# Pacing the preparation of a batch by the steps of the batch before it

## The chip, the core and the metric

The kernel runs on one core of a Trainium2 chip. The metric is device time in microseconds (us); lower is better. A time is the median of several runs; the profile is of one more execution of the same program.

## The reference: what is computed

The input is x of shape 4 x 128 x 64 x 64: four batches, 128 channels, 4096 positions, in float32. Two layers follow each other.

Layer 0 normalizes x in groups, derives offsets and a mask for 9 taps per position from a 3 x 3 convolution, samples the image bilinearly at the offset places (a deformable convolution), multiplies with a weight, and adds the result to x.

Layer 1 treats the 4096 positions as tokens of 128 features. After a layer norm, each of 16 heads of width 8 forms cosines and their running products; these features are query, key and value at once:

```python
scores = jnp.einsum('bhsd,bhtd->bhst', q, q) / np.sqrt(D)
attn = jax.nn.softmax(scores, axis=-1)
ctx = jnp.einsum('bhst,bhtd->bhsd', attn, q)
```

A projection, a small feed-forward network and a mixture of 8 experts (2 taken per token) follow, each with a residual. Batches don't depend on each other. Within a batch, attention needs the features of all its positions.

## The kernel before

**The main work is a list of steps.** The 16 heads are 4 groups of 4, the 4096 queries 8 chunks of 512, the 4096 keys 32 tiles of 128. A run is one batch, group and query chunk; a step is one key tile of a run. `scores` (line 1170) issues four matmuls (L1178, PE) into two PSUM tiles `sc` and two exponentials (L1187, ACT) from there into two tiles `e`. `context` (line 1191) multiplies `e` with the values into the accumulator `acc` (L1195, PE). Scores are issued two steps ahead of the context (`LAG`). Tag `sc` has 3 buffers of two PSUM banks, tag `e` has 6 in SBUF, which is three steps. Scores of two chunks against each other are symmetric, so some `e` tiles are transposed on DVE (`turn`, L1069), stored, loaded as `et` and used in a later run (L1131) in place of new scores. There are 964 steps for batch 0, and 4 x (8 x 32 - 7 x 4) = 912 for each of batches 1 to 3, so 3700 in all, with 7400 exponentials; the batches end at steps 964, 1876, 2788 and 3700 (`of_batch`, line 1260).

**Beside the steps run three kinds of jobs**, written as Python generators. "prepare" (line 785) makes a batch ready: group norm, a table of image corners in DRAM, offsets, then `deform` (line 563), and with it `convolved` and `features`, which are also named "prepare". "finish" (line 1012) does all that follows attention for one chunk. "turned" adds the `et` products. The generators run at build time: each `yield need(pe, dve, lat, ...)` (line 197) says what the next piece will cost on PE and DVE and how long to wait after it. `Beside` (line 62) is a planner with its own clock, which advances 1.82 us per step (`STEP`); at each step it takes pieces from its queue, sorted by rank (lowest first), until the planned PE credit (0.44 us per step, at most one PE piece per step) or the DVE backlog (3.2 us, or 0.4 near the end of a run) is used up. The order it finds is the order of the instructions on PE, DVE, SP and POOL, which each run theirs in that order. ACT holds the exponentials and few others. A `yield` itself emits no instruction.

**`deform` works through 96 units**: 8 chunks of positions x 3 groups of taps x 4 blocks of 128 positions. A unit takes a tile `v` that three indirect DMAs on POOL (L575) have gathered (three `v` buffers; two units are gathered ahead), multiplies and adds it on DVE (L589, L591, L592), transposes three blocks on DVE into `tr` (L617), and issues the gathers of the unit after next. The four units of a tap group share a `tr` tile, which lies in one of the three buffers `st` that `turn` uses too; after the fourth, four DMAs on SP store it (`smd<-tr`). After 12 units, `convolved` loads the chunk again (12 DMAs `sT<-smd` on SP) and multiplies it with the weight in 18 PE pieces (`conv_ps`, L273), and `features` writes keys, queries and values to DRAM. `progress[b]` (line 584) is 0.1 + 0.9 x the share of units begun.

**What orders "prepare" against the rest.** When a batch begins, "prepare" of the next is added, with `begun` the step at which that happens (lines 1371 to 1374); for batch 1 it is a step of batch 0 after the preparation of batch 0 itself, near step 288. At each step the main loop (line 1330) compares `progress` of the coming batch with `share`, the part of the steps that have passed out of those up to 80 before the batch's end, and sets the rank of all "prepare" jobs:

```python
share = (n - begun) / (of_batch[b] - 80 - begun)
beside.rank("prepare", 2 if progress.get(b + 1, 0.0) > share else 0.5)
```

"finish" has rank 1 (a second one beside it 2) and "turned" -1. So a preparation that is ahead of its share comes behind "finish", and one that is late comes before it; one that is ahead still runs whenever there is room. On the first step of a batch's last run, all that is left of "prepare" is emitted at once (`drain`, line 1379). `force` (line 156) takes "prepare" pieces when no score can be issued because keys are missing.

**When "finish" has work.** Batches 0 and 1 run group by group over all 8 chunks, so a chunk is complete only in the last quarter of the batch; much of "finish" falls into the next batch. Batch 2 is in two halves of 4 chunks and batch 3 goes chunk by chunk (`LOTS`, line 44).

Of the kernel before, what the change touches and what calls it, by code (L numbers as in the profile page):

```python
# [196 lines left out]
def need(pe=0.0, dve=0.0, lat=0.0, hold=False, after=0.0):  # L197

    return pe, dve, lat, hold, after


def ve(n, ops=1):

    return ops * (0.17 + n / 960.0)
# [6 lines left out]
def tr(n):  # L213

    return 0.13 + 0.115 * n
# [3 lines left out]
def kernel(  # L219
# [37 lines left out]
    prepared = {}  # L257

    progress = {}
    featuring = []  # L260


# [2 lines left out]
    def misc(name):  # L265
        if alone:
            return ps_s.tile([P, 2, 512], F32, tag="sc", name=name)[:, 0, :]
        return ps_m.tile([P, 512], F32, tag="misc", name=name)
# [294 lines left out]
    def deform(b, tab, idx, wt):  # L563


        AHEAD = NV - 1
        units = [
            (ch, kg, j) for ch in range(NCH) for kg in range(3) for j in range(4 * ch, 4 * ch + 4)
        ]

        def gather(_, kg, j):
            v = work.tile([P, 3, 4 * C], F32, tag="v", name=f"v{b}_{j}_{kg}", bufs=NV)
            for k in range(3):
                kk = 3 * kg + k
                nc.gpsimd.indirect_dma_start(  # L575
                    out=v[:, k, :], out_offset=None, in_=tab,
                    in_offset=bass.IndirectOffsetOnAxis(ap=idx[:, j, kk : kk + 1], axis=0),
                )
            return v, beside.gathered()

        sent = 0.0
        ahead = [gather(*units[n]) for n in range(AHEAD)]
        for n, (ch, kg, j) in enumerate(units):
            progress[b] = 0.1 + 0.9 * n / len(units)
            v, landed = ahead.pop(0)
            v4 = v.rearrange("p k (q c) -> p (k q) c", c=C)
            w12 = wt[:, j, 3 * kg : 3 * kg + 3, :].rearrange("p k q -> p (k q)")
            yield need(dve=ve(1536), after=landed)
            nc.vector.tensor_tensor(v4, v4, w12[:, :, None].to_broadcast([P, 12, C]), ALU.mult)  # L589
            yield need(dve=ve(768) + ve(384))  # L590
            nc.vector.tensor_tensor(v[:, :, : 2 * C], v[:, :, : 2 * C], v[:, :, 2 * C :], ALU.add)  # L591
            nc.vector.tensor_tensor(v[:, :, :C], v[:, :, :C], v[:, :, C : 2 * C], ALU.add)  # L592
            if (b, ch) == (0, 0):

                if (kg, j) == (0, 0):
                    sT = big.tile([P, KK, CH], F32, tag="xs", name="sT_first")
                yield need(pe=tr(3), dve=ve(384))
                pt = misc(f"sT_ps{j}_{kg}")
                for k in range(3):
                    nc.tensor.transpose(pt[:, P * k : P * (k + 1)], v[:, k, :C], ident)  # L600
                nc.vector.tensor_copy(
                    sT[:, 3 * kg : 3 * kg + 3, P * j : P * (j + 1)],
                    pt[:, : 3 * P].rearrange("p (k c) -> p k c", c=P),
                )
                if n + AHEAD < len(units):
                    beside.later(beside.dve, lambda u=units[n + AHEAD]: ahead.append(gather(*u)))
                if (kg, j) == (2, 3):
                    featuring.append(True)
                    beside.add("prepare", convolved(b, ch, sT), 0.5, True)
                continue  # L610

            yield need(dve=ve(384))
            if j % 4 == 0:
                beside.flush(sent)
                tr9 = work.tile([P, 4, 4, 4, 32], F32, tag="st", name=f"tr{b}_{ch}_{kg}", bufs=NST)
            for k in range(3):
                nc.vector.transpose(  # L617
                    out=tr9[:, k, :, j % 4, :],
                    in_=v[:, k, :C].rearrange("p (c i) -> p c i", i=32),
                )  # L620
            if n + AHEAD < len(units):
                beside.later(beside.dve, lambda u=units[n + AHEAD]: ahead.append(gather(*u)))
            if j % 4 < 3:
                continue
            while kg == 0 and len(featuring) > 1:
                yield need(lat=1.0)

            def put(ch=ch, kg=kg, tr9=tr9):
                for o in range(4):
                    nc.sync.dma_start(  # L630
                        out=smd[ch % 2][:, 3 * kg : 3 * kg + 3, :, o].rearrange(
                            "i k c n -> i (k c) n"
                        ),
                        in_=tr9[32 * o : 32 * (o + 1), :3].rearrange("p k c j t -> p (k c) (j t)"),
                    )

            sent = beside.dve
            beside.later(sent, put)
            if kg == 2:

                while featuring:
                    yield need(lat=1.0)
                featuring.append(True)
                beside.later(
                    beside.dve + 0.1,
                    lambda ch=ch: beside.add("prepare", convolved(b, ch), 0.5, True),
                )
        while featuring:
            yield need(lat=1.0)
# [135 lines left out]
    def prepare(b):  # L785
        xs = big.tile([P, KK, CH], F32, tag="xs", name=f"xc{b}")
        xc = xs.rearrange("p k n -> p (k n)")[:, :NPOS]
        for i in range(4):
            nc.sync.dma_start(
                out=xc[:, 1024 * i : 1024 * (i + 1)], in_=xf[b, :, 1024 * i : 1024 * (i + 1)]  # L790
            )
        tab = tabs[b % NTAB]
        if b == 1:
            borders(tab, nc.sync)
        yield need(lat=8.0)
        got = []
        yield from group_norm(b, xc, got)
        yield from corner_table(b, xc, *got, tab)
        idx = work.tile([P, NBLK, KK], I32, tag="idx", name=f"idx{b}", bufs=1)
        wt = work.tile([P, NBLK, KK, 4], F32, tag="wt", name=f"wt{b}", bufs=1)  # L800
        yield from offsets(b, xc, idx, wt)
        if b == 0:
            settle()
        yield from deform(b, tab, idx, wt)
# [289 lines left out]
    def granted(emit):  # L1094
        if room[0]:
            room[0] -= 1
            emit()
        else:
            asking.append(emit)
# [7 lines left out]
    def fetch(run, kt):  # L1107
        giver = takes[run]
        g, par = runs[giver][1], runs[giver][2] % 2
        if (g, par, kt) in turning:  # L1110
            beside.flush()
        e = turned_tile(run, kt)
        nc.sync.dma_start(
            out=e.rearrange("p r h x -> p (r h x)"),
            in_=etd[g][par][kt].rearrange("p r x -> p (r x)"),
        )
        fetched[run, kt] = e, beside.now + 16.0
# [44 lines left out]
    def load_queries(run):  # L1162
        b, g, sc = runs[run][:3]
        if run not in queries and (b, sc) in prepared:
            q = work.tile([P, CH], F32R, tag="qT", name=f"qT{run}", bufs=3)
            nc.sync.dma_start(out=q.bitcast(F32), in_=qTd[b % 2][sc][P * g : P * (g + 1)])
            queries[run] = q
            landing[run] = beside.now + 4.0
# [91 lines left out]
    of_batch = {runs[i][0]: ends[i + 1] for i in range(len(runs))}  # L1260
# [4 lines left out]
    for n, (run, t) in enumerate(steps):  # L1265
        b, g, sc = runs[run][:3]
# [54 lines left out]
    n = issued = begun = 0  # L1321
    beside.rate = 1.0
    with tc.manual_schedule(engines={PE, DVE, SP, POOL}):
# [6 lines left out]
        while n < len(steps):  # L1330
# [11 lines left out]
            b, g, sc, ts, kind = runs[run]  # L1342
# [10 lines left out]
                backlog = 0.4 if at >= len(ts) - 3 else 3.2  # L1353
            if b + 1 < NB:

                share = (n - begun) / (of_batch[b] - 80 - begun)
                beside.rank("prepare", 2 if progress.get(b + 1, 0.0) > share else 0.5)
            beside.step(backlog)
            if issued <= n + LAG and issued < len(steps) and at_hand(issued, n):
# [2 lines left out]
            if t == ts[0]:  # L1362
# [8 lines left out]
                if not beside.has("prepare") and b + 1 < NB and (b + 1, 0) not in prepared:  # L1371
                    beside.rate = beside.RATE
                    begun = n
# [2 lines left out]
                beside.drain("turned")  # L1376
            if following:
                if following[0] != b and at == 0:
                    beside.drain("prepare")

                if at == 1:
                    load_queries(run + 1)
                    if len(ts) <= 8 and run + 2 < len(runs):
                        load_queries(run + 2)
                if run + 1 in takes and at == len(ts) - 5:
                    for kt in range(4):
                        granted(lambda r=run + 1, kt=kt: fetch(r, kt))
# [91 lines left out]
```

## Time and profile before

| | |
|---|---|
| time before, median of 3 runs | 7759.71 us (7757.02 to 7764.04) |
| profiled execution | 7737.5 us |
| its span, first to last instruction | 7735.7 us |
| mean granted TensorE clock | 0.964 |
| PE busy | 7156.1 us, 93% |
| ACT busy | 6871.2 us, 89% (of it the exponentials 6868.1) |
| DVE busy | 4484.8 us, 58% |
| POOL busy | 1648.3 us, 21% (of it the gathers 1444.7) |

Busy time is the union of an engine's instructions; the busy time of PE is modelled from pipelined matmuls, so it is no measure of how much room PE has. A group line of the profile names line, engine, operation, what is written and read, the count, the busy time and the mean duration, and behind the bar the idle time of the engine just before those instructions and what ended most of it. A window line gives start and end in us from the span's start, its length, then for each engine asked for the busy time and the count, the granted TensorE clock (1.00 is full speed), the busy share of the 16 DMA engines and GB/s.

### The profile page before, as it was taken

What the parts mean: (1) busy time and instruction counts of PE and PEld (TensorE: products, weight loads), DVE (VectorE), ACT (ScalarE), POOL (GpSimd) and SP (SyncE); (2) the same over time, 40 slices, a digit from 0 to 9 for tenths busy, and PEclk for the clock granted to TensorE, in tenths of its full rate; (3) what the DMA queues carried; (4) which work ended last, traced back from release to release, by engine and by line L of the source; (5) the groups of instructions that cost most, each with busy time, mean ns of one, the idle gap of its engine ahead of it and who ended that gap; (6) DMA issues with size and microseconds to landing.
All of it is one profiled execution on the core that took longest, in us unless ns stands there. A gap on an engine that the chain in (4) does not pass through costs nothing.

```text
span 7735.7 us, 181988 instructions
## 1 busy us (share of the span) xinstructions
PE 7156.1 (93%) x73700; PEld 2517.5 (33%) x73700; DVE 4484.8 (58%) x9000; ACT 6871.2 (89%) x7441; POOL 1648.3 (21%) x1326
## 2 busy tenths in 40 slices
PE   2579999899999999999999989989999999999997
PEld 1122232323333333333333323333333333333333
DVE  7666456666444767776554667765444545545444
ACT  0478999888999899989999988988999999999995
POOL 5454134343000432422000333431000000000000
PEclk6789999999999999999999999999999999999998
DMA  5777567978556878887766788997665587777762
GB/s 175 207 229 229 145 202 236 306 240 282 162 169 198 277 226 269 280 268 247 206 177 184 236 259 281 295 296 248 183 188 161 150 253 242 245 236 253 240 216 76
DMA packets 928758, 1735.41 MB, mean 224 GB/s; under 512 B 169458, under 2 KB 398348, under 8 KB 877228
## 3 DMA queue, kind: packets, MB, share of 16 engines
q1 hardware_dynamic: 828062, 1417.20, 60.4%
q0 software_dynamic: 92160, 302.06, 12.1%
q8 instruction: 578, 9.47, 0.5%
q10 hardware_dynamic: 7694, 4.52, 0.2%
q14 instruction: 264, 2.16, 0.1%
HBM read 1061.47 MB, written 661.93 MB: 223 GB/s over the span
## 4 chain that ended last, share of the span: by engine, by line
PE 81%; DMA 7%; DVE 4%; issue 2%; ACT 2%; SPq 2%; another core or an unknown queue 0%; POOL 0%; ACTq 0%; POOLq 0%; DVEq 0%
PE acc L1195 39%; PE sc L1178 24%; PE acc L1131 5%; PE e_ps L273 4%; PE conv_ps L273 3%; ACT e L1187 2%; PE f_ps L273 2%; DMA sT<-smd 1%; DMA et<-etd 1%; PE om_ps L507 1%; DMA etd<-st 1%; DVE v L589 1%; DMA kT<-kTd 1%; DMA qT<-qTd 1%; PE ao_ps L273 1%
## 5 line engine op out<-in xcount | busy, mean ns | idle before, releaser
L1187 ACT ACTIVATE e<-sc 128x1024 f32<-128x1024 f32 x7400 | 6868.1, 1068 | 724.7 <-PE sc L1178 470.2
L1195 PE MATMUL acc<-e,qf 128*32 128x512 f32 x29600 | 3961.1, 605 | 27.0 <-DVE cu L1399 16.2
L1178 PE MATMUL sc<-qT,kT 32*128 32x512 f32 x14800 | 2390.7, 500 | 292.4 <-ACT e L1187 153.6
L1178 PEld LDWEIGHTS sc<-qT,kT 32*128 32x128 f32 x14800 | 956.3, 183 | 3697.6 <-ACT e L1187 3078.1
L575 POOL DMA_INDIRECT v<-tab,idx x1152 | 1444.7, 1254 | 1754.5 <-DVE tr L617 1108.1
L1069 DVE STREAM_TRANSPOSE st<-e 128x1024 f32<-128x1024 f32 x792 | 937.4, 1222 | 775.5 <-ACT e L1187 606.5
L1195 PEld LDWEIGHTS acc<-e,qf 128*32 128x32 f32 x29600 | 800.4, 110 | 587.7 <-issue 329.1
L376 POOL TENSOR_TENSOR r<-ln_t,expo 128x4 f32<-128x4 f32 x96 | 112.2, 1169 | 3135.1 <-DVE ln_t L374 3096.3
L589 DVE TENSOR_TENSOR v<-v,wt 128x1536 f32<-128x1536 f32 x384 | 666.0, 1734 | 91.3 <-DMA v<-tab,idx 63.2
L1131 PE MATMUL acc<-et,qf 128*32 128x128 f32 x12672 | 521.3, 281 | 36.4 <-DMA et<-etd 30.5
L993 DVE TENSOR_TENSOR eo<-e_ps,gt 128x512 f32<-128x512 f32 x256 | 175.1, 685 | 549.6 <-PE e_ps L273 544.2
L273 PE MATMUL conv_ps<-sT,wconv_sb 128*32 128x256 f32 x4464 | 365.9, 402 | 26.4 <-DMA sT<-smd 17.9
L1131 PEld LDWEIGHTS acc<-et,qf 128*32 128x32 f32 x12672 | 302.4, 110 | 236.8 <-issue 187.1
L591 DVE TENSOR_TENSOR v<-v 128x768 f32<-128x768 f32 x384 | 367.9, 958 | 10.5
L1397 DVE COPY cu<-acc 128x512 f32<-128x512 f32 x128 | 88.5, 691 | 413.7 <-PE acc L1195 372.0
L617 DVE STREAM_TRANSPOSE tr<-v 128x128 f32<-128x128 f32 x1116 | 257.7, 282 | 40.4 <-DMA etd<-st 25.1
L592 DVE TENSOR_TENSOR v<-v 128x384 f32<-128x384 f32 x384 | 215.5, 561 | 13.3
L376 POOL TENSOR_TENSOR rstd<-lt_t,expo 128x4 f32<-128x4 f32 x32 | 57.7, 1804 | 533.2 <-DVE lt_t L374 526.2
L273 PE MATMUL f_ps<-w_sb,h 128*32 128x128 f32 x4096 | 164.8, 280 | 0.0
L878 DVE TENSOR_SCALAR h<-h_ps,b_sb 128x512 f32<-128x512 f32 x128 | 95.0, 744 | 102.5 <-PE h_ps L876 99.1
L273 PEld LDWEIGHTS conv_ps<-sT,wconv_sb 128*32 128x32 f32 x4464 | 91.4, 109 | 170.1 <-issue 151.3
L754 POOL COPY fx<-rn 128x512 f32<-128x512 f32 x32 | 28.9, 904 | 528.9 <-DVE rn L753 328.1
(224 smaller groups left out, 3041.1 us busy)
## 6 DMA issues: line engine op xcount, KB each, us to landing
etd<-st SPq DMA_DIRECT2D x1584, 256.0 KB
et<-etd SPq DMA_DIRECT2D x396, 1024.0 KB
kT<-kTd SPq DMA_DIRECT2D x400, 256.0 KB
smd<-tr SPq DMA_DIRECT2D x372, 192.0 KB
sT<-smd SPq DMA_DIRECT2D x372, 192.0 KB
qf<-fqd SPq DMA_DIRECT2D x400, 144.0 KB
qT<-qTd SPq DMA_DIRECT2D x166, 256.0 KB
atd<-cu SPq DMA_DIRECT2D x128, 256.0 KB
```

The lines of the kernel that those rows point to most:

```text
L273: nc.tensor.matmul(dst[c : c + 32], lhsT=lhsT[:, c : c + 32], rhs=rhs, start=start, stop=stop)
L575: nc.gpsimd.indirect_dma_start(out=v[:, k, :], out_offset=None, in_=tab, in_offset=bass.IndirectOffsetOnAxis(ap=idx[:, j, kk : kk + 1], ax ...
L589: nc.vector.tensor_tensor(v4, v4, w12[:, :, None].to_broadcast([P, 12, C]), ALU.mult)
L591: nc.vector.tensor_tensor(v[:, :, : 2 * C], v[:, :, : 2 * C], v[:, :, 2 * C :], ALU.add)
L592: nc.vector.tensor_tensor(v[:, :, :C], v[:, :, :C], v[:, :, C : 2 * C], ALU.add)
L617: nc.vector.transpose(out=tr9[:, k, :, j % 4, :], in_=v[:, k, :C].rearrange("p (c i) -> p c i", i=32),)
L993: nc.vector.tensor_tensor(ws[hf], pe.rearrange("p (e c) -> p e c", c=C), gt[:, i, 4 * hf : 4 * (hf + 1), None].to_broadcast([P, 4, C]), AL ...
L1069: nc.vector.transpose(out=st[:, :, 2 * pr : 2 * pr + 2, :].rearrange("p o h (q j) -> p o (h q) j", j=32), in_=es[pr].rearrange("p h (q o i ...
L1131: nc.tensor.matmul(acc[32 * h : 32 * (h + 1), P * kt : P * (kt + 1)], lhsT=qf[:, t, QW * h : QW * h + 32], rhs=e[:, :, h, 32 * t : 32 * (t ...
L1178: nc.tensor.matmul(ps[i // 2][:, i % 2, :], lhsT=kT[h : h + 32, P * (t % 4) : P * (t % 4 + 1)], rhs=qT[h : h + 32, :], start=True, stop=True,)
L1187: nc.scalar.activation(e, ps[pr], AF.Exp, scale=1.0 / math.sqrt(HD))
L1195: nc.tensor.matmul(acc[32 * h : 32 * (h + 1), :], lhsT=qf[:, t % 4, QW * h : QW * h + 32], rhs=es[h // 2][:, h % 2, :], start=(t == ts[0]) ...
```

## The change

A list `due` of one number is added. At each step the main loop writes the current `share` into it, and `share` now counts up to 200 steps before the end of the batch in place of 80. At the head of each unit, `deform` of batches 1 to 3 asks whether its progress is more than 0.06 above `due[0]`; while it is, it yields a piece without work that is ready again 1.5 us later on the planner's clock. Before the draining at the last run of a batch, `due[0]` is set to 1.

```diff
     progress = {}
+
+    due = [1.0]
     featuring = []
...
         for n, (ch, kg, j) in enumerate(units):
             progress[b] = 0.1 + 0.9 * n / len(units)
+            while b and progress[b] > due[0] + 0.06:
+                yield need(lat=1.5)
             v, landed = ahead.pop(0)
...
             if b + 1 < NB:

-                share = (n - begun) / (of_batch[b] - 80 - begun)
+                share = (n - begun) / (of_batch[b] - 200 - begun)
+                due[0] = share
                 beside.rank("prepare", 2 if progress.get(b + 1, 0.0) > share else 0.5)
...
                 if following[0] != b and at == 0:
+                    due[0] = 1.0
                     beside.drain("prepare")
```

## Prediction

> **What bounds the kernel now.** I read the page first: which engine is filled, and when.
>
> ```profile
> span 7735.7 us, 181988 instructions
> ...
> ACT  0478999888999899989999988988999999999995
> ...
> L1187 ACT ACTIVATE e<-sc 128x1024 f32<-128x1024 f32 x7400 | 6868.1, 1068 | 724.7 <-PE sc L1178 470.2
> ```
>
> ACT has 7400 exponentials at 6868.1 / 7400 = 0.928 us, 1.856 us per step, and little else. After the start the time is therefore 1.85 us per step plus whatever ACT idles. ACT's row in the slices drops from 9 to 8 in three places; the windows of the exponentials (start:end, length, ACT busy, count, clock, DMA share, GB/s) say how much:
>
> ```profile
> 987.00:2007.00 1020.00, 910.85 (x980) 0.97 0.81 251
> 2007.00:2292.00 285.00, 284.43 (x309) 1.00 0.56 165
> 2292.00:3668.00 1376.00, 1257.60 (x1353) 0.98 0.81 251
> 3668.00:4105.00 437.00, 436.32 (x473) 1.00 0.65 187
> 4105.00:5384.00 1279.00, 1126.65 (x1209) 0.98 0.84 261
> 5384.00:7600.00 2216.00, 2204.05 (x2385) 1.00 0.70 214
> ```
>
> Length minus busy is ACT's idle time: 109.2, 0.6, 118.4, 0.7, 152.4 and 12.0 us. The same windows for the units' first multiplication (L589) have 96, 0, 96, 0, 96 and 0 of them: ACT idles only while a preparation is under way, 380 us in three stages, which I call stages 1, 2 and 3 (for batches 1, 2 and 3). "finish" and the turned products do it no harm alone.
>
> Next, who holds ACT up in stage 3 (the waits of ACT in that window: total, times, longest):
>
> ```profile
> ACT e L1187 <- PE acc L1195: 65.1, 57, 2.7
> ACT e L1187 <- PE sc L1178: 55.8, 46, 5.2
> ```
>
> PE, in two ways. The timeline shows the first:
>
> ```profile
> 4474.73 1.94 ACT L1187 ACTIVATE e<-sc 128x1024 f32<-128x1024 f32 x2 [1.16 <-PE acc L1195]
> ...
> 4476.24 0.64 PE L273 MATMUL conv_ps<-sT,wconv_sb 128*32 128x256 f32 x8
> ...
> 4476.70 1.04 PE L1195 MATMUL acc<-e,qf 128*32 128x512 f32 x8
> ...
> 4477.84 1.94 ACT L1187 ACTIVATE e<-sc 128x1024 f32<-128x1024 f32 x2 [1.16 <-PE acc L1195]
> ```
>
> A step takes 4477.84 - 4474.73 = 3.11 us, because the exponential starts when `acc` of two steps earlier ends (4476.70 + 1.04 = 4477.74). It lasts some steps, costs about 1.2 us each, and is gone. Counted over the trace, starts within 0.2 us after that end hold 45, 46 and 66 us of the three stages' idle time. My reading, an inference: with three steps' worth of `e` this happens when a turned `e` is freed late because DVE's queue is deep. The rest are late scores behind PE's waits for DMAs and DVE.
>
> **How near the limit lies.** The new head of a unit emits no instruction: the program keeps its 181988 instructions in another order. Unit k (0 to 95) may begin when 0.1 + 0.9 k/96 <= (n - begun)/(end - 200 - begun) + 0.06. For stages 2 and 3, begun and end are 912 steps apart, so n >= begun + 712 x (0.04 + 0.009375 k) = begun + 28 + 6.675 k. Where the units stand now follows from the first and last start of L589 (1062.9 and 1926.0; 2491.6 and 3602.5; 4324.5 and 5290.9) and half the exponentials counted up to there:
>
> - Stage 1: begun about 288, 476 steps in place of 712, so unit 0 from step 307 and unit 95 from 731. Now they run at 718/2 = 359 and 359 + 815/2 = 766: some 35 steps or more behind the limit. It never binds. No "finish" work exists before the last quarter of batch 0, so the rank decides nothing: **0 us**.
> - Stage 2: begun 964. Unit 0 runs at 964 + 204/2 = 1066 (limit 992), unit 95 at 1066 + 1080/2 = 1606 (limit 1626). Only the last chunks bind, by up to 20 steps.
> - Stage 3: begun 1876. Unit 0 at 1876 + 226/2 = 1989 (limit 1904), unit 36 at 1989 + 328/2 = 2153 (limit 2144), unit 95 at 2153 + 558/2 = 2432 (limit 2538). From about unit 36 the limit binds, and at the end the preparation is 106 steps later, still 250 steps ahead of the batch; no draining, no forced pieces.
>
> **What the moved work meets.** Held are, for some 60 units of stage 3: three POOL gathers each (1.25 us), 1.74 + 0.95 + 0.56 + 3 x 0.28 = 4.1 us of DVE, every fourth unit 4 SP stores, and per chunk 12 SP loads, 144 `conv_ps` matmuls and the DVE work of the features. Nothing on an engine's queue waits for a held unit, as the hold is in the order and not on the chip; SP and POOL get these DMAs later among the others, each behind the DVE work that it stores or frees, as now; the held buffers are two `v` (nobody else's by then) and one of three `st`, now for 3 x 6.7 = 20 steps in place of 14, and stage 2 already holds it 17. DVE's idle time before turning in stage 3 for a store of `tr` was 33.3 us over 160 transposes and is not ACT's: I take 0, and 33 us as the bad end.
>
> The price of the pace comes from comparing stages. These are the windows of ACT for units 0 to 35 and 36 to 95, stage 3 and then stage 2:
>
> ```profile
> 4324.00:4680.00 356.00, 305.88 (x328) 0.97 0.84 263
> 4680.00:5291.00 611.00, 520.73 (x558) 0.97 0.90 290
> 2491.00:2916.00 425.00, 380.59 (x410) 0.98 0.80 251
> 2916.00:3602.00 686.00, 623.37 (x671) 0.98 0.88 277
> ```
>
> | | steps per unit | ACT idle | per unit | per step |
> |---|---|---|---|---|
> | stage 3, first 36 | 4.6 | 50.1 us | 1.39 | 0.31 |
> | stage 3, last 60 | 4.65 | 90.3 us | 1.50 | 0.32 |
> | stage 2, first 36 | 5.7 | 44.4 us | 1.23 | 0.22 |
> | stage 2, last 60 | 5.6 | 62.6 us | 1.04 | 0.19 |
>
> Stage 1, with 96 units in 407 steps (4.2 each), idled 105.0 us there, 1.09 per unit, but had no "finish" beside it. So idle time is neither fixed per step nor quite per unit. At the slower pace it is lower per unit. For the 60 held units, then 6.4 steps apart, I take stage 2's 1.04 in place of 1.50: 62.6 - 90.3 = **-28 us**. Bounds: no gain per unit, 0; no idle time left at all, -90. The 106 steps into which the work moves have ACT full now (91.27 of the 93 us after 5291) and must take part of this idle time; the per-unit figure contains that.
>
> Rank: with 200, a preparation counts as late for longer, so in stage 2 it goes before "finish" more often (unit 12 is at its share at step 1115, under the old rule at 1141). "finish" then ends later, and the stretch after it, 3668 to 4105 with 0.7 us idle, hides that. I take 0; if the cover were gone, the price is the difference between the parts of stage 2, (1.23 - 1.04) x 36 = 7 us either way.
>
> Sum: 0 + 0 - 28 + 0 = -28 us: 7737.5 - 28 = 7709.5 for the profiled execution, which is 22 us under the median shown; on the median 7759.7 - 28 = **7732 us**, -0.36%.
>
> Two rules of the Trainium skill speak against more than that. The gap of 1.16 us repeats exactly; "Perfetto Trace Analysis", section "Optimization Strategy", says consistent bubbles can mean too few buffers for the next tile. By that rule the gaps would follow the turned tiles, whose number stays, and the gain would be 0. The clock rows are 0.97 in 4680 to 5291 and 1.00 after; "TensorE: Matmul & The Clock Gate", section "HAM oscillation — how this bites in real kernels", says that idle gaps of PE above about 3.4 us throttle it again. If a longer stage kept 0.97, 106 steps at 1.86 us would lose 3%, 6 us, and the sum would be -22.
>
> **The rivals.**
>
> 1. *The idle time is per unit, and the order is only dealt anew.* For it: stage 1, the fastest, has no more per unit than stage 2. Against: stage 3 has 40% more. Gives 0, with some 10 us either way from the new order.
> 2. *Slower: the idle time is per step that a preparation is alive.* Each step then has turning, stores and a deep DVE queue beside it; "finish" takes the DVE room that held units leave, since the planner fills its backlog with any ready job. Price: 106 steps x 0.32 + 20 x 0.19 = +38 us, in stage 3 between steps 2153 and 2538, so 7798. It decides if held units idle more than 90.3 / 385 = 0.23 us per step; stage 2 measured 0.19, stage 3 0.32. For it: most idle time is with `conv_ps` or `et` on PE, which remain. Against: stage 2.
> 3. *A larger gain.* The planner's backlog stays low whenever a unit is held, turned tiles are freed in time, and the 3.11 us steps go: up to -90, so 7670.
> 4. *The change doesn't do what it says*: the limit doesn't bind. True of stage 1 and most of stage 2; for stage 3 the step numbers exclude it. It belongs with rival 1.
>
> **How the numbers follow.** This kernel's measurement can tell about 0.2%, 15.5 us, from no change. Forecast (-16 to -60): 0.38. Larger gain (rival 3): 0.12. Rivals 1 and 4: 0.27. Rival 2: 0.23. So faster 0.50, same 0.27, slower 0.23. Likeliest own range 7700 to 7744. The range takes in most of rivals 2 and 3: 7670 to 7803; the 33 us for `st` lies within it.
>
> **What would show it.** The first 2000 us as before. In stage 3, L589 from about 4325 to 5470, unit starts 6.7 steps apart, POOL's gathers thinned out likewise; ACT idle in the last 60 units near 60 us; steps of 3.11 us fewer in stage 3 and as many in stage 2. Wrong: idle time per unit of 1.5 or more at the slower pace, idle time of ACT after 5500 us or between 3668 and 4105, or stage 1 changed.

## The result, and the profile after

| | before | after |
|---|---|---|
| median of 20 runs each | 7751.22 us (7734.60 to 7772.24) | 7775.64 us (7760.84 to 7802.88) |
| ratio after / before, 95% interval | | 1.0033 (1.0025 to 1.0041) |
| profiled execution | 7737.5 us | 7776.7 us |

The changed kernel is 24 us slower; 7732 was forecast. The profiled execution of before lies 14 us under its median and that of after on its own, so the two traces are 39 us apart, 15 more than the medians; a second pair, below, is 48 us apart. First the page of after:

```profile
span 7774.9 us, 181967 instructions
...
ACT  0478999888999898889999988889999999999995
...
L1191 ACT ACTIVATE e<-sc 128x1024 f32<-128x1024 f32 x7400 | 6867.8, 1067 | 769.0 <-PE sc L1182 504.9
```

The exponentials take what they took (6868 us); ACT's idle time before them has grown from 724.7 to 769.0 us, so all of it is waiting. Which stage? The windows of ACT after, cut at the same steps as those shown of before (320, 810, 964, 1640, 1876, 2480), the last one cut again at step 2800:

```profile
992.00:2016.00 1024.00, 911.14 (x983) 0.98 0.80 250
2016.00:2306.00 290.00, 284.81 (x312) 0.99 0.55 163
2306.00:3704.00 1398.00, 1257.99 (x1360) 0.98 0.80 249
3704.00:4148.00 444.00, 436.15 (x476) 0.99 0.63 179
4148.00:5410.00 1262.00, 1126.49 (x1216) 0.97 0.82 254
5410.00:6016.00 606.00, 592.04 (x644) 1.00 0.65 198
6016.00:7643.00 1627.00, 1612.59 (x1759) 1.00 0.73 225
```

Length minus busy: 112.9, 5.2, 140.0, 7.9, 135.5, 14.0, 14.4 us, against 109.2, 0.6, 118.4, 0.7, 152.4 and, for what is now two windows, 12.0. The pace came as computed: in stage 3 the units stand 6.57 steps apart from unit 36 on (4.73 before), and the last L593 (the units' first multiplication, L589 before) starts at step 2538, 5531 us. Stage 3 moved 17 us of idle time out of its first part (8 in a second pair of traces) and has 14 back in the next window, which had none. **The loss is in stage 2**, where I had put 0: 22 us in its main window and 7 in the one behind it.

The waits of ACT in stage 3 (4148 to 5540), against 65.1 and 55.8 us before, say that the kinds of waiting are the same:

```profile
ACT e L1191 <- PE acc L1199: 63.2, 53, 2.6
ACT e L1191 <- PE sc L1182: 51.4, 52, 6.0
```

**How far one trace goes.** Between steps 320 and 810 the order is the same in both kernels and in most of those below; ACT's idle time there was 109 and 121 us in two traces of before, 113 and 131 in two of after, and up to 132 in others. Traces of one and the same order thus lie up to 23 us apart there, and a difference below some 20 us in one stage of one trace is no finding by itself. The experiments ran on several chips, which fall into two kinds: on some the kernel before takes 7749 to 7777 us (that of the result too, and those of the first eight runs below), on others 7610 to 7613. Between the kinds only ratios to the kernel before on the same chip are compared.

### The profile page after: what moved, and what is told of

Same layout as the page of the kernel before. It is cut to its first block, busy times and chain, and to the rows that moved or that the text cites. A ratio compares the mean times of both kernels' runs of the same rounds, so it can differ in the third digit from the quotient of the medians.

```text
span 7774.9 us, 181967 instructions
## 1 busy us (share of the span) xinstructions
PE 7182.2 (92%) x73700; PEld 2520.8 (32%) x73700; DVE 4481.9 (58%) x9000; ACT 6871.1 (88%) x7441; POOL 1602.5 (21%) x1326
## 4 chain that ended last, share of the span: by engine, by line
PE 82%; DMA 6%; DVE 4%; ACT 3%; issue 2%; SPq 2%; another core or an unknown queue 0%; ACTq 0%; POOL 0%; POOLq 0%; DVEq 0%
PE acc L1199 40%; PE sc L1182 24%; PE acc L1135 5%; PE conv_ps L275 4%; PE e_ps L275 3%; ACT e L1191 3%; PE f_ps L275 2%; DMA et<-etd 1%; PE om_ps L509 1%; DMA sT<-smd 1%; DMA qT<-qTd 1%; DMA etd<-st 1%; DVE v L593 1%; DVE st L1073 0%
## 5 line engine op out<-in xcount | busy, mean ns | idle before, releaser
L1191 ACT ACTIVATE e<-sc 128x1024 f32<-128x1024 f32 x7400 | 6867.8, 1067 | 769.0 <-PE sc L1182 504.9
L577 POOL DMA_INDIRECT v<-tab,idx x1152 | 1393.3, 1209 | 1872.3 <-DVE tr L621 1191.6
L593 DVE TENSOR_TENSOR v<-v,wt 128x1536 f32<-128x1536 f32 x384 | 666.7, 1736 | 91.6 <-DMA v<-tab,idx 68.3
```

The lines of the kernel that those rows point to most:

```text
L577: nc.gpsimd.indirect_dma_start(out=v[:, k, :], out_offset=None, in_=tab, in_offset=bass.IndirectOffsetOnAxis(ap=idx[:, j, kk : kk + 1], ax ...
L1191: nc.scalar.activation(e, ps[pr], AF.Exp, scale=1.0 / math.sqrt(HD))
```

## The experiments

In the tables, "stage 2" and "stage 3" are ACT's idle time (us) in steps 964 to 1876 and 1876 to 2800, the quieter steps behind a preparation included; "end" is 2800 to 3700, "tail" the time from the last exponential to the last instruction. All these are counted over the traces.

**Which part of the change?** Four kernels on one chip (before: 7748.8 us); end220 and a second trace of before and of after on another (before: 7777.3).

hold_alone: the hold as in the change, the rank by 80 as before.

```diff
-share = (n - begun) / (of_batch[b] - 200 - begun)
-due[0] = share
+share = (n - begun) / (of_batch[b] - 80 - begun)
+due[0] = (n - begun) / (of_batch[b] - 200 - begun)
```

> The hold as in the change, but the rank of the preparation still by the share up to 80 steps before the end. Three theories of the 25 us that the change costs. Rank: in stage 2 the preparation now goes before the finishing work, and this is what costs; then stage 2 idles 114 to 120 us on ACT as before and the kernel is within 10 us of before. Alive: idle time is paid per step that a preparation lives; then the same life gives +20 to +30 us. Order: the time hangs on which pieces happen to meet in the new order; then stage 2 and stage 3 may each differ from before and from the change by 10 to 25 us, without a rule.

stage3_alone: hold and rank only for the preparation in stage 3.

```diff
-share = (n - begun) / (of_batch[b] - 200 - begun)
-due[0] = share
+share = (n - begun) / (of_batch[b] - (200 if b == 2 else 80) - begun)
+due[0] = share if b == 2 else 9.0
```

> Rank and hold changed for the preparation of batch 3 alone; batches 1 and 2 as before. Rank: within 10 us of before, since stage 3 was never ranked differently for long. Alive: +20 to +35 us, as the 106 added steps are all in stage 3. Order: stage 2 equal to that of before (118 us idle on ACT, within 8), stage 3 within 20 us of that of before, so -15 to +20 in all.

end80: both, with 80 for 200, so the hold binds harder (units of stage 3 are 7.8 steps apart) and binds in stage 1 too (5.6 in place of 4.4). end220: with 220.

```diff
-share = (n - begun) / (of_batch[b] - 200 - begun)
+share = (n - begun) / (of_batch[b] - 80 - begun)     # end220: 220
```

> The hold with the old 80 in place of 200 in the share, so that the units of stages 2 and 3 are 7.8 steps apart and the preparations end 130 and 220 steps later than before. Alive: 130 x 0.19 + 220 x 0.27 = +80 us or more over before. Per unit (the forecast's rival 1): 0 to +25 us. The forecast's own mechanism (less idle time per unit at a slower pace): below 0. Rank: the rank rule is that of before, so near 0.

> The change with 220 in place of 200: the units of stages 2 and 3 are 6.5 steps apart in place of 6.7, and all pieces meet anew. If the time follows the pace (200: +25 us, 80: -7 to -15), it is at +25 to +30. If it follows the chance of the order, it lies anywhere from -20 to +35, and probably not within 5 us of the change.

slack07: the margin 0.07 in place of 0.06.

```diff
-            while b and progress[b] > due[0] + 0.06:
+            while b and progress[b] > due[0] + 0.07:
```

> The change with 0.07 in place of 0.06, which moves the limit of each unit some 7 steps earlier. Alive and rank: within 6 us of the change, so +18 to +32 us over before. Order: another order, so it may lie 10 to 25 us from the change on either side, with other steps slow.

before_again and after_again: the two kernels unchanged.

> The kernel before once more, for a second profile. It says how far two executions of one program differ in each stage. If the stages' idle times on ACT (109, 118 and 152 us) come back within 5 us, a difference of 20 us between two programs in one stage means something; if they scatter by 20 us, it does not.

> The changed kernel once more, for a second profile. In the first one, from the start of batch 1 to step 1876 ACT idled 30 us more than in the kernel before, and in stage 3 about as much. If the order of stage 2 is the cause, its surplus of 20 us or more comes back; if it was chance of one execution, it shrinks under 10 us.

| | ratio to before | stage 2 | stage 3 | end | tail |
|---|---|---|---|---|---|
| before, two traces | 1 | 119, 129 | 153, 150 | 11, 14 | 80, 81 |
| after, two traces | 1.0033 (1.0025 to 1.0041) | 148, 160 | 150, 156 | 15, 17 | 76, 75 |
| hold_alone | 1.0041 (1.0026 to 1.0056) | 124 | 167 | 9 | 103 |
| stage3_alone | 1.0000 (0.9990 to 1.0009) | 124 | 147 | 14 | 81 |
| end80 | 0.9980 (0.9968 to 0.9993) | 115 | 109 | 15 | 137 |
| slack07 | 1.0013 (1.0003 to 1.0024) | 127 | 159 | 3 | 89 |
| end220 | 0.9988 (0.9977 to 0.9998) | 146 | 141 | 4 | 80 |

What follows: paced in stage 3 alone, the change neither costs nor gains. The slowest pace, end80, is the fastest kernel, so a slower pace as such does not cost: my rival 2, idle time per step that a preparation is alive, is out. A gain below the kernel before is what the forecast's own mechanism said of end80; that one order was run at this pace, so the pace and the luck of its order are not told apart. Neither does the rank decide by itself: with the rank of before (hold_alone) stage 2 is as before and the kernel loses 32 us elsewhere; slack07 has the rank of 200 and, in its one trace, a good stage 2 too; and end220, 20 steps from the change, turns +24 us into -9. That the rank plays a part in stage 2 is not excluded: in the table, the kernels ranked by 200 or 220, all but slack07, have more idle time there than those ranked by 80. The small steps from 0.06 to 0.07 and from 200 to 220 move the time as much as the change did, without direction. The planner finds another order each time.

**Is it the deep DVE queue?** shallow_dve is the kernel before with DVE's backlog at 1.6 in place of 3.2, after my inference that turned `e` are freed late.

```diff
-backlog = 0.4 if at >= len(ts) - 3 else 3.2
+backlog = 0.4 if at >= len(ts) - 3 else 1.6
```

> The kernel before with the planner's limit on the DVE backlog at 1.6 us in place of 3.2; nothing else. My theory of the 3.11 us steps is that a turned tile is freed late behind a deep DVE queue, so that an exponential gets the buffer of two steps earlier and waits for acc. With a shallower queue such waits must become fewer: from 160 us of idle time in the three stages to 110 us or less, and the time falls by 30 to 60 us if nothing else gets late. If the repeated gap only comes from having six e buffers, it stays near 160 us.

7920.73 us, ratio 1.0181 (1.0167 to 1.0195), where 30 to 60 us less was expected. ACT's waits for `acc` did fall, from 157.5 to 91.5 us, which supports the inference; but those for `sc` rose from 470.2 to 571.9, and the tail from 80 to 215 us, most of the loss; I put that down to "finish", which finds less room beside the steps. The deep queue costs waits and buys more than they cost.

**What is lost in stage 2.** Most gaps of ACT of 2.5 us or more sit at the same steps in each trace of the changed kernel: 9 of the 11 in stage 2 come back in its second trace (3 of 5 in those of before). In stage 2 they sum to 26.0 and 35.4 us before, and to 56.1 and 64.7 after, 30 us more: the loss. At step 1127 the timeline of after reads (lines not needed are left out):

```profile
2619.71 0.34 SPq L1117 DMA_DIRECT2D et<-etd  x1
...
2622.20 0.52 SPq L1034 DMA_DIRECT2D a<-rdd  x1
...
2629.26 1.08 PE L1135 MATMUL acc<-et,qf 128*32 128x128 f32 x16 [4.56 <-DMA et<-etd]
2629.62 0.69 DVE L833 TENSOR_TENSOR aT<-aT,a 128x512 f32<-128x512 f32 x1 [14.20 <-DMA a<-rdd]
...
2630.11 1.94 PE L1199 MATMUL acc<-e,qf 128*32 128x512 f32 x8
...
2634.22 2.33 DVE L1073 STREAM_TRANSPOSE st<-e 128x1024 f32<-128x1024 f32 x2
...
2635.52 4.90 ACT L1191 ACTIVATE e<-sc 128x1024 f32<-128x1024 f32 x5 [8.72 <-DVE st L1073]
```

Two loads issued 2.5 us apart are used 9.5 and 7.4 us after their issue, as soon as they have landed. PE's next piece waits for `et` (4.56 us), with `acc` and the next scores behind it. DVE's next piece, a "finish" multiplication that the planner allows 6 us after the issue of `a`, has waited 14.20 us, with turning and the multiplications of a unit behind it; the turned `e` comes free at 2635.5, and ACT has stood 8.72 us.

The windows of PE there show two things that the timeline does not (after the busy time and the count: the granted clock, the share of the DMA engines, GB/s):

```profile
2619.70:2629.20 9.50, 5.01 (x68) 0.95 1.05 317
2628.30:2635.00 6.70, 5.74 (x52) 0.50 0.29 109
```

From the issue of `et` to its use the 16 DMA engines were busy throughout (share 1.05, which can pass 1 as a packet counts where it begins; 0.80 over the stage's main window), and the granted clock of PE fell to half, from 2628.2 to 2635.1. Of the seven stalls of 4 us or more in stage 2 of this trace, five (1127, 1268, 1411, 1466, 1491) came after 8 us with a share of 1.04 to 1.08, and those at 1696 and 1032 after 0.94 and 0.49; some 35% of all stretches of 8 us in the stage have more than 0.95. So the stalls go with full DMA engines; that these cause them is not shown.

At step 1411 it is `et` again (6.54 us of PE), at 1696 `a` through `aT` (PE 5.26 us), at 1466 a turn that waits 8.73 us for the store of the `st` tile. DVE's waits for the two small loads of "finish" over the whole run, after and then before:

```profile
DVE aT L833 <- DMA a<-rdd: 79.0, 15, 14.2
...
DVE rd L1029 <- DMA rd<-atd: 55.2, 15, 12.1
```

```profile
DVE aT L829 <- DMA a<-rdd: 53.5, 14, 12.0
DVE rd L1025 <- DMA rd<-atd: 36.0, 10, 10.0
```

no_sums_after and no_sums_before take these two waits away and keep the order of every engine: "finish" computes with tiles that are there, so the softmax isn't normalized.

```diff
-nc.vector.tensor_tensor(aT, aT, a4.rearrange("p i c -> p (i c)"), ALU.mult)
+nc.vector.tensor_tensor(aT, aT, r.rearrange("p i c -> p (i c)"), ALU.mult)
...
-nc.sync.dma_start(out=rd, in_=rows[:, HD].rearrange("h (q n) -> h q n", q=HD))
+rx_ = work.tile([P, CH // HD], F32, tag="rx_", name=f"rx_{b}_{ch}")
+nc.sync.dma_start(out=rx_, in_=rows[:, HD].rearrange("h (q n) -> h q n", q=HD))
...
-nc.vector.reciprocal(rd, rd)
+nc.vector.reciprocal(rd, vec_sb[:, 1, : CH // HD])
```

> The changed kernel with the order of every engine kept, but 'finish' no longer reads what its two small loads bring: the reciprocal takes a constant tile of ones in place of the loaded sums, and aT is multiplied with the residual r in place of the loaded reciprocals a (so the softmax isn't normalized; all loads and stores are still issued). Two of DVE's waits are gone: aT <- DMA a<-rdd (79.0 us, 15 times in the changed kernel, 53.5 before) and rd <- DMA rd<-atd (55.2 us, 53 in number of tenths before: 36.0). Theory (landings): the stage-2 stalls of ACT in the changed kernel are a PE piece or a turning on DVE queued behind a DMA that lands later than the planner counted; those at steps 1127 (8.8 us), 1491 (4.9) and 1696 (6.7) go back to these two loads, so they vanish and the time falls by 18 us (10 to 30), more than the same edit takes from the kernel before. Rival (the order alone, the loads are bystanders): within 5 us of the changed kernel, the stalls at these steps remain.

> The same edit on the kernel before (softmax not normalized, loads and stores still issued, order of all engines kept). Theory (landings): before has no stall of ACT above 2.5 us in stage 2 that goes back to these two loads (its large ones are a transposed tile's load at 1581 and convolution input at 1491), so it falls by 0 to 10 us, and the difference of after and before shrinks from 25 us to 5 to 15. Rival: both fall alike or not at all, and the difference stays at 25 us.

These two and the next two were the first on a chip of the other kind (before: 7610.3 us). After the edit the changed kernel has 0.9962 (0.9948 to 0.9976) of the time of before, 7581.2 us, and the kernel before 0.9980 (0.9971 to 0.9989), 7596.4 us: 15 us the other way round. Unedited, the changed kernel has 0.9996 on such chips (third_after, below), so the edit took some 26 us from it and 15 from the kernel before. The stalls at 1491, 1696 and also 835 are gone, to 0.0 us, but a new one of 9.7 us stands at 1497; that at 1127 stays, at 10.1 us, so I had put it down to the wrong one of its two loads.

late_sums_after and late_sums_before leave the computation whole and tell the planner that the two loads land later: 8 us for 4, and 14 for 6.

```diff
-        yield need(lat=4.0)
+        yield need(lat=8.0)
...
+        yield need(lat=8.0)
         yield from attention_out(b, ch, r, aT, a4)
```

> The changed kernel, with the planner told that the two loads land later: 8 in place of 4 us for the sums, 14 in place of 6 us for the reciprocals. Nothing else is edited; the order of the work changes by it from the first 'finish' on, about step 800. Theory (landings): DVE's waits aT <- DMA a<-rdd fall from 79.0 to under 25 us and rd <- DMA rd<-atd from 55.2 to under 30; the time falls by about 15 us against the changed kernel, with some 15 us either way from the new order. Rival (order alone): the waits fall too, but the time moves by up to 25 us either way without regard to them.

> The kernel before with the same two figures of the planner. Theory (landings): its waits for the two loads (53.5 and 36.0 us) fall in the same way; the time is 5 us lower, with some 15 us either way from the new order, and lies within 15 us of the changed kernel with the same figures. Rival: the two differ by 25 us or more either way.

0.9985 (0.9976 to 0.9994) and 1.0055 (1.0042 to 1.0069). The waits for `a` fell to 24.0 and 8.2 us, those for `rd` to 27.9 and 30.7. Against its 0.9996 on such chips the changed kernel gained some 8 us, with intervals that overlap, where about 15 was expected; the kernel before lost 42 us, about 20 of them in stage 2 (waits for `acc` of two steps earlier) and 22 in the tail (80 to 102 us). The waits for a landing are one way to lose time; the new order finds others. This pair speaks for my rival 1 as much as for the loads.

**What is different on the other chips.** The kernel before, same instructions, 140 us faster: where? third_after, before_third and end80_again are the changed kernel, the one before and end80 once more, all three on such chips.

> The changed kernel once more, beside the kernel before. If this chip shows the unexplained delays after gathers (kernel before near 7750 to 7780 us, some 120 such delays or more between steps 320 and 2800): theory 'delays' says 25 us slower (20 to 40), with more of the delays than before. If it shows few (kernel before near 7610): theory 'delays' says 10 to 20 us faster than before, as the pair without the loads of the sums differed by 15; theory 'landings' (the single stalls at fixed steps are the loss) says 15 to 25 us slower on any chip.

> The changed kernel with 80 in place of 200 in the share, once more (7741.56 against 7751 the first time, ratio 0.998). Both theories: faster than before by 10 to 40 us; 'delays' expects the larger gain on a chip with few of them, since end80 lost 200 us to them between steps 0 and 2800 as against 162 of the kernel before, and lost 41 us less to waits for the freeing of e.

> The kernel before, one execution for its trace. On a chip with few delays (near 7610 us): against the changed kernel's trace of the same kind, stage 3 (steps 1876 to 2800) loses 15 to 30 us more to idle ACT and stage 2 (964 to 1876) 15 to 25 us less, so that the sum is equal. On a chip with many (near 7750 to 7780): 120 or more delays between steps 320 and 2800, and the losses as in its two traces so far.

| chip with before at 7610 to 7613 us | ratio to before | stage 2 | stage 3 | end | tail |
|---|---|---|---|---|---|
| before_third | 1 | 78 | 115 | 9 | 80 |
| no_sums_before | 0.9980 | 79 | 125 | 4 | 77 |
| third_after | 0.9996 (0.9986 to 1.0005) | 101 | 94 | 18 | 75 |
| no_sums_after | 0.9962 | 92 | 101 | 10 | 72 |
| end80_again | 0.9923 (0.9910 to 0.9937) | 67 | 50 | 13 | 136 |

Here **the change makes no difference**: 7609.98 us beside 7612.95. Neither theory had this: the delays beside gathers (below) said 10 to 20 us faster, the stalls at fixed steps 15 to 25 us slower. The four windows of ACT (stage 1, stage 2, stage 3, end) of before_third and of third_after:

```profile
959.00:2232.00 1273.00, 1193.46 (x1293) 0.97 0.76 238
2232.00:4001.00 1769.00, 1691.02 (x1835) 0.99 0.78 242
4001.00:5832.00 1831.00, 1715.58 (x1859) 0.99 0.77 240
5832.00:7505.00 1673.00, 1664.01 (x1814) 1.00 0.72 222
```

```profile
963.00:2252.00 1289.00, 1194.22 (x1293) 0.97 0.76 235
2252.00:4044.00 1792.00, 1690.85 (x1835) 0.98 0.78 239
4044.00:5852.00 1808.00, 1713.77 (x1858) 0.99 0.79 243
5852.00:7535.00 1683.00, 1664.93 (x1815) 1.00 0.71 220
```

Stage 2 loses 23 us, as on the other kind (its stalls of 2.5 us or more: 24.8 us before, 57.5 after, most at the same steps). Stage 3 gains 21 us, which it did not on the chips above; the expectation of before_third, made after the trace of third_after, had both. The first window's 15 us are spread: between steps 320 and 810, in one and the same order, nine traces on these chips have 79 to 99 us.

What these chips lack shows in the timeline of before on a chip of the slower kind, at step 416. One run of 16 identical matmuls on loaded weights breaks into pieces behind a gather on POOL, for no wait that the trace knows, and ACT stands 1.81 us:

```profile
1184.92 1.47 POOL L575 DMA_INDIRECT v<-tab,idx  x1 [0.30 <-issue]
...
1184.98 0.42 PE L1131 MATMUL acc<-et,qf 128*32 128x128 f32 x7
...
1185.56 0.42 PE L1131 MATMUL acc<-et,qf 128*32 128x128 f32 x3 [0.16 <-issue]
...
1186.28 0.43 PE L1131 MATMUL acc<-et,qf 128*32 128x128 f32 x5 [0.29 <-issue]
...
1187.02 0.28 PE L1131 MATMUL acc<-et,qf 128*32 128x128 f32 x1 [0.31 <-issue]
```

I counted exponentials between steps 320 and 2800 that started late though their scores were done for over 0.25 us and `acc` of two steps earlier did not release them: 122 and 137 before, 147 and 152 after, 1.1 to 1.3 us each, over 90% of them during a gather or within 2 us after its end (against some 30% of all exponentials); on the faster chips 21 and 19, hardly nearer to gathers than others. They hold 138 and 161 us before, 166 and 204 after on the slower chips, and there another 24 to 29 us before step 320; on the faster chips 22 and 42, and none before step 320. So they are most of the 140 us between the kinds. The 22 and 42 are a few long stalls of the order that the count takes in; less these, stage 2 has 43 us of delays before and 41 after (means of two traces), stage 3 45 before and 58 after. Per step of a preparation under way that is 0.10 in stage 3 before (443 steps) and 0.11 after (549 steps), so there they go with the steps. That explains 13 of the 22 us by which stage 3 fares worse on the slower kind; the rest is within the spread.

plain_after and plain_before replace each indexed gather by a plain DMA from POOL, from fixed rows (the samples are then not those of the offsets).

```diff
-nc.gpsimd.indirect_dma_start(out=v[:, k, :], out_offset=None, in_=tab,
-    in_offset=bass.IndirectOffsetOnAxis(ap=idx[:, j, kk : kk + 1], axis=0))
+nc.gpsimd.dma_start(out=v[:, k, :], in_=tab[256 * kk : 256 * (kk + 1), :].rearrange("(p two) c -> p (two c)", two=2))
```

> The changed kernel with each indexed gather replaced by a plain DMA on POOL of the same size from fixed rows of the same table (so the samples are not those of the offsets); the order of every engine is kept. Theory 'delays': on a chip with many of them they fall from about 150 to under 30 between steps 320 and 2800 and the time by 100 to 190 us against the changed kernel, unless plain DMAs from POOL cause the same delays, in which case nothing moves; on a chip with few, within 25 us. Theory 'landings': no such fall; within 20 us.

> The same replacement in the kernel before. Theory 'delays': on a chip with many delays it falls by 80 to 150 us, less than the changed kernel does, so that the difference of the two closes from 25 us to 5 or turns. Theory 'landings': the difference stays 25 us.

> The kernel before with plain DMAs on POOL from fixed rows in place of the indexed gathers (so the samples are not those of the offsets; the order is kept), once more. If this chip shows the delays in the kernel before: theory 'the indexed gathers cause them' says they fall from 120 or more to under 30 and the time falls by 80 to 150 us; rival 'any DMA from POOL, or something else of that chip' says within 25 us. On a chip without them: within 15 us, as the first time.

1.0006 (0.9996 to 1.0015), 0.9991 (0.9981 to 1.0001) and, again, 0.9998 (0.9988 to 1.0008): all three on chips without the delays, where the theory of the delays expects nothing. The 25 us between the two kernels that the theory of the landings expected did not come (11 and 6 us). Inconclusive: that the gathers cause the delays is a coincidence in time, counted, and not shown. The three traces do repeat the two stages of the faster chips: stage 2 has 102 us in plain_after and 79 and 79 in plain_before, stage 3 98 against 112 and 122.

**The best version** is end80, 0.9980 and 0.9923 (7554.8 us) on the two kinds. On the page of end80_again ACT's slices are 9 from the fourth to the last but one:

```profile
span 7552.5 us, 181942 instructions
...
ACT  0479999999999999999999999999999999999992
```

Its tail is 56 us longer than before; that much would be left to gain.

## Why the prediction was wrong, point by point

- **What bounds the kernel** held: ACT's idle time beside preparations makes the difference between all these kernels, besides the tail.
- **How near the limit lies** held to the step: stage 1 unbound, stage 2 only in its last chunks (unit 95 at 1631; 1605 before; limit 1626), stage 3 from unit 36 (2151, 2538).
- **The price of the pace failed**, the one term of the sum that was not 0: "For the 60 held units, then 6.4 steps apart, I take stage 2's 1.04 in place of 1.50: 62.6 - 90.3 = -28 us." The held units now idle 99.4 and 98.8 us where they idled 90.0 and 87.7 on the result's kind of chip, 1.66 a unit; 67.0 for 75.0 on the other kind. That is +10 and -8, not -28. At this pace the difference between stages 2 and 3, from which I took the price, does not follow the pace: the first 36 units of stage 3, which kept theirs, gained as much or more (50.4 and 50.9 to 41.3 and 46.3 us, 38.4 to 26.0) in their new order. Rival 1 was right on this: per unit, the order dealt anew. Only its spread, "some 10 us either way", was too small: neighbours of the change lie from -15 to +32 us by their ratios. That a slower pace never helps is not shown: in end80, at 7.8 steps a unit, the last 60 units of stage 3 idle 67.1 us, and 27.7 on the faster kind; but in its stage 2, at 7.7 steps, they idle 68.4 and 43.3, where before has 62.6, 69.8 and 49.5.
- **Stage 2 and the rank, put at 0**, with 7 us either way, failed as well, and this is where the time is lost: +29 and +31 us of idle time, +23 on the faster chips. It lies in the last 60 units (88.5 and 91.8 us against 62.6 and 69.8), so the 1.04 per unit that I took as the price of a slow pace rose to 1.5 in stage 2 itself. I gave cover for a later end of "finish" (the stretch 3668 to 4105) and none for what a new order puts next to each other. The cover failed too: 7.9 us of idle time there in place of 0.7. About 9 of the 23 us went with the two loads of "finish" (101 to 92 us, while the kernel before stayed at 78 and 79), in one trace each; the rest looks to be stalls behind `et` and `st`, seen in the timeline and not taken away one by one.
- **"Nothing on an engine's queue waits for a held unit"** held, but I looked only at the held work and not at the pieces that move into its place. The 33 us for `st` was the right kind of term, a DVE queue behind a DMA, and in the wrong stage.
- **Rival 2** (idle time per step that a preparation is alive, +38) is refuted as a whole by end80 and by stage3_alone, though the mark that I had set for it came: the held units idle 99.4 us in 387 steps, 0.26 us per step, over 0.23. On the slower chips a part of the idle time, the delays beside gathers, does behave so, for 13 us.
- **Consistent bubbles.** The rule of the Trainium skill ("Perfetto Trace Analysis", section "Optimization Strategy") that gaps that repeat can mean too few buffers gave 0 for the starts that wait for `acc` of two steps earlier. They hold 66.1 us of stage 3 before and 66.5 after, as that rule said; but in end80 25.7, with the same buffers, so the number of buffers does not set them alone.

What I had listed as signs of being wrong came: idle time per unit above 1.5, and idle time between 3704 and 4148 and after 5500. The measured 7776 us lies within the range of 7670 to 7803, but its upper part was there for rival 2 and for a wait on `st` in stage 3, and neither is what happened: that is luck.

On the result's kind of chip the account is then, as the mean of two pairs of traces: stage 2 +30, stage 3 +1 (the gain of the other kind less the delays and the spread), the steps from 320 to 964, in one order up to 810, +11, start, end and tail a few us either way, +44 in all; the medians differ by 24. On the faster kind, one pair: stage 2 +23, stage 3 -21, steps 320 to 964 +15, start +4, end and tail +4, +25 in all; the medians differ by -3. So 20 to 28 us of what the traces differ by belongs to the executions traced, and the account by stages is no closer than that. What stays open is what causes the delays beside gathers, why one order meets more late landings than another, and whether a pace as slow as that of end80 gains by itself.

## What to carry to other kernels

Where a build-time planner deals the order of in-order queues, a change of one number deals the whole order anew; before explaining a difference of 0.3%, run two or three neighbouring numbers and see how far they scatter, then choose among them by measurement. A price per unit read from two stages of one trace mixes the pace with the order of each stage and is no price. In the trace, tell the single stalls that come back at fixed steps, which here went with the order, from those that change from run to run or are missing on another chip, and count them apart before looking for a cause.

## What the runs showed of the hardware

- **The same program differs by 2% between chips** (7749 to 7777 and 7610 to 7613 us), at nearly the same granted clock (0.964 and 0.966). Most of it is interruptions of PE and ACT of 1.1 to 1.3 us that come with gathers on POOL on one kind and not on the other. A change of 0.3% had one sign on one kind and none on the other.
- **A stall costs more than its wait.** After PE's 4.56 us at step 1127, the 16 `et` matmuls took 1.08 us in place of 0.64 and the 8 of `acc` 1.94 in place of 1.04, at a granted clock of 0.50. Counted over nine traces from the faster chips, `acc` is slow (over 1.6 us) in all 57 cases after an idle time of PE of 5 us or more, in 78% of 18 after 2.8 to 3.4 us and in 63% of 16 after 2.0 to 2.4, and in 22% of 40 after 0.8 to 1.2. All 329 slow `acc` of these traces between steps 320 and 2800 lie in a stretch with the clock at 0.5; of the others 69 in some 22,000 do. The Trainium skill, "TensorE: Matmul & The Clock Gate", section "HAM oscillation — how this bites in real kernels", gives about 3.4 us as the idle time to stay under. The runs agree that longer gaps slow PE, and show it often for gaps of 2 us: after 10 of the 16 gaps of 2.0 to 2.4 us the clock was at 0.5.
- **A small load can land late.** `a<-rdd` was used 7.4 us after its issue at step 1127, shortly after an `et` of 1 MB had been issued and with the DMA engines full (share 1.05), where the planner counted 6; DVE's longest wait for it in the run was 14.2 us, and in third_after 17.2.
